# A diffusion and expert kernel on one core: inverse roots by Newton's steps, the first pair of tiles projected ahead of the edges, two PSUM banks for the first layer

## The chip, the cores and the metric

The kernel runs on one core of a Trainium2 chip. The metric is the device time of one execution in microseconds (us), less being better. A core has five engines with a queue each: TensorE (PE in the profile, with PEld for its weight loads), VectorE (DVE), ScalarE (ACT), GpSimd (POOL) and SyncE (SP), which issues transfers. An engine works through its own queue in order and waits for the others by semaphores.

## What is computed

x has 3125 rows of 256 numbers, and a graph of 103,125 edges joins the rows. The first half normalises each row, sends it through a linear layer, a silu, six steps of averaging over the graph and a second linear layer; the second half is a mixture of eight experts with two chosen for each row.

```python
x = x + gnn(layernorm(x), src, dst)      # first half
#   h = silu(layernorm(x) @ W_in.T + b_in)
#   term = h; out = h
#   for i in 1..6:  term = inv_deg * segment_sum(term[src], dst) / i;  out += term
#   gnn = out @ W_out.T + b_out
x = x + moe(layernorm(x))                # second half: top 2 of 8 experts
```

The averaging is linear, so the kernel applies W_out ahead of it: it diffuses rows of 256 already projected numbers, t0.

## The kernel before

The rows lie in 25 tiles of 128 (`NT`, the last one with 53 rows). The work has these stages.

*Prologue, to 96 us.* It has two strands that share all engines. The edges' strand takes source and destination of every edge (`si`, `di`, loaded on ACT's queue), turns them into three small numbers (`part`, L417 to L427), transposes them on PE (L433), copies them out of PSUM (`pairs`, L436 and L437) and writes them to DRAM (`edges`, two writes from ACT's queue, L439 and L441). POOL gathers, by indirect transfers, a row of destinations for each group of rows (`row_i`, L455) and then the edges of the group (`rec`, L471). From these, DVE and ACT work out where each row's edges begin (L474 to L506), the inverse degrees (L510 to L515, the last of it five multiplications on POOL), and the two arrays `place` and `lane` (L527 to L536) from which the adjacency blocks are made. The rows' strand normalises x and projects it. x comes by SP's queue in five pieces (L322), tiles 0 to 1, 2 to 5, 6 to 11, 12 to 17 and 18 to 23. Mean and variance are taken on DVE (L556, L557); the inverse root is ACT's Sqrt (L558) and DVE's reciprocal (L559), in three batches: tiles 0 to 1, 2 to 5, 6 to 24. Sqrt and silu need different tables in ACT, and a table load stands in ACT's queue where the function changes. Then come 13 pairs of tiles: `xn` on ACT (L567), four transposes on PE into `pt` (L572), `xt` copied out by ACT (L579), `ph` = the first layer in two halves on PE (L586), each followed by a silu on ACT into `ht` (L588), `pm` = the output layer on PE (L593), and `t0` in two parts on DVE, the high part rounded to the fp32r type (L595) and what is left of it (L596). `ph` and `pm` have one buffer each, `pt` two. The xn of the next pair is written ahead of the present pair's layers.

*Step 1.* For each of the 25 destination tiles a dense block of the adjacency matrix is built: DVE makes one-hot arrays `left` (L638) and `right` (L647), PE multiplies them into `pa` (L658, 40 matmuls a block), ACT copies `pa` into `blk` (L662), SP writes the block to DRAM. 25 matmuls of the block with t0 then give the tile's sum `pd` (L703). The first blocks' one-hot matmuls are interleaved with the projection; the first L703 needs the whole t0.

*Steps 2 to 6, the router and the experts* load the blocks again (L1014) and do the second half (L954, L963). They begin after step 1.

The source's order sets each engine's queue, except that the scheduler which builds the program moves instructions between strands within each engine by its own estimate of when their inputs are ready; `tc.issue_after(x)`, which the changed kernel uses, holds what is written under it behind instruction x in that order. The projection's loop, which the change rewrites, is in the function printed below.

Of the kernel before, what the change touches and what calls it, by code (L numbers as in the profile page):

```python
# [10 lines left out]
F32 = mybir.dt.float32  # L11
F16 = mybir.dt.float16
F32R = mybir.dt.float32r
BF16 = mybir.dt.bfloat16
I32 = mybir.dt.int32
U32 = mybir.dt.uint32
AF = mybir.ActivationFunctionType
ALU = mybir.AluOpType
AX = mybir.AxisListType

P = 128
N = 3125
D = 256
NT = 25
# [3 lines left out]
NCH = (NE + P - 1) // P  # L28
# [4 lines left out]
STEPS = 6  # L33
# [3 lines left out]
EPS = 1e-5  # L37
# [3 lines left out]
NG = NT * P // W // 2  # L41
# [225 lines left out]
def tile_gnn_then_moe(  # L267
# [20 lines left out]
    nc = tc.nc  # L288

    const = ctx.enter_context(tc.tile_pool(name="const", bufs=1))  # L290
    work = ctx.enter_context(tc.tile_pool(name="work", bufs=2))
# [9 lines left out]
    prep = before.enter_context(tc.tile_pool(name="prep", bufs=1))  # L301
# [2 lines left out]

    acc = const.tile([P, NT, D], F32, name="acc")
    nc.vector.memset(acc[:, NT - 1, :], 0.0)
    first_i = prep.tile([NG, NCH], I32, name="first_i")
    di = prep.tile([P, NCP], I32, name="di")
    nc.scalar.dma_start(di, dst_pm)
    w_in_sb = const.tile([P, 2, D], F32, name="w_in_sb")  # L310
    nc.scalar.dma_start(w_in_sb, w_in.rearrange("(k p) o -> p k o", p=P))
    si = prep.tile([P, NCP], I32, name="si")
    nc.scalar.dma_start(si, src_pm)
    b_in_pm = const.tile([P, 2], F32, name="b_in_pm")
    for c in range(2):
        nc.scalar.dma_start(b_in_pm[:, c:c + 1], b_in[c * P:(c + 1) * P].rearrange("(p a) -> p a", a=1))
    w_out_sb = const.tile([P, 2, D], F32, name="w_out_sb")
# [3 lines left out]
    for a, b in ((0, 2), (2, 6), (6, 12), (12, 18), (18, 24)):  # L321
        nc.sync.dma_start(acc[:, a:b, :], x[a * P:b * P, :].rearrange("(t p) d -> p t d", p=P))  # L322
        if a == 0:
            nc.sync.dma_start(first_i, bass.AP(tensor=dst_pm.tensor, offset=dst_pm.offset,
                                               ap=[[0, NG], [1, NCH]]))
    for p in (0, HP):
        nc.sync.dma_start(acc[p:p + LAST, NT - 1, :], x[(NT - 1) * P:N, :])

    ident = const.tile([P, P], F32, name="ident")
    make_identity(nc, ident)  # L330
    eps_sb = const.tile([P, 1], F32, name="eps_sb")
    nc.vector.memset(eps_sb, EPS)
    inv_deg = const.tile([P, STEPS, NT], F32, name="inv_deg")
    big = const.tile([1, 1], I32, name="big")


# [6 lines left out]
    t0 = evens.enter_context(tc.tile_pool(name="even", bufs=1, side="right")).tile(  # L343
        [P, NT, 2 * D], F32R, name="t0")
# [33 lines left out]
    low = keys.tile([NG, 2], F32, name="low")  # L378
# [33 lines left out]
    nc.vector.tensor_copy(ident_h, ident)  # L412


    cb = (NCP + P - 1) // P
    part = prep.tile([P, 3, NCP], F16, name="part")
    nc.vector.tensor_scalar(part[:, 2, :], di, -MID, None, op0=ALU.add)  # L417
# [10 lines left out]
    pairs = prep.tile([P, cb, P, 3], F16, name="pairs")  # L428
    for v in range(3):
        pq = ps.tile([P, 1024], F16, name="pk")[:, :cb * P].rearrange("p (c e) -> p c e", e=P)  # L430
        for c in range(cb):
            n = min(P, NCP - c * P)
            nc.tensor.transpose(pq[:n, c, :], part[:, v, c * P:c * P + n], ident_h)  # L433
        n = NCP - (cb - 1) * P
        put = nc.vector.tensor_copy if v == 1 else nc.scalar.copy
        put(pairs[:, :cb - 1, :, v], pq[:, :cb - 1, :])  # L436
        put(pairs[:n, cb - 1, :, v], pq[:n, cb - 1, :])  # L437
    by_chunk = edges.rearrange("(c p) v -> c p v", p=P)
    nc.scalar.dma_start(by_chunk[:(cb - 1) * P].rearrange("(b c) p v -> c b p v", c=P),  # L439
                        pairs[:, :cb - 1])  # L440
    nc.scalar.dma_start(by_chunk[(cb - 1) * P:], pairs[:NCP - (cb - 1) * P, cb - 1])  # L441


    junk = prep.tile([P, NCH], BF16, name="junk")
    below = prep.tile([NG, 2], F32, name="below")
    for g in range(2):
        nc.vector.tensor_scalar(junk[:NG, :], first_i, low[:, g:g + 1], None, op0=ALU.is_lt,
                                op1=ALU.add, accum_out=below[:, g:g + 1])
    chunk = prep.tile([NG, 2], F32, name="chunk")
    nc.vector.tensor_scalar(chunk, below, -1.0, 0.0, op0=ALU.add, op1=ALU.max)  # L450
    chunk_i = prep.tile([NG, 2], U32, name="chunk_i")
    nc.vector.tensor_copy(chunk_i, chunk)
    row_i = prep.tile([NG, 2, P], I32, name="row_i")
    for g in range(2):
        nc.gpsimd.indirect_dma_start(  # L455
            row_i[:, g, :], None, dst_cm,
            bass.IndirectOffsetOnAxis(ap=chunk_i[:, g:g + 1], axis=0))
    within = prep.tile([NG, 2], F32, name="within")
    for g in range(2):
        nc.vector.tensor_scalar(junk[:NG, :P], row_i[:, g, :], low[:, g:g + 1], None,  # L460
                                op0=ALU.is_lt, op1=ALU.add, accum_out=within[:, g:g + 1])
    start_i = prep.tile([NG, 2], U32, name="start_i")
    nc.vector.scalar_tensor_tensor(start_i, chunk, float(P), within, op0=ALU.mult, op1=ALU.add)

# [5 lines left out]
    for g in range(2):  # L470
# [4 lines left out]
                                op0=ALU.subtract, op1=ALU.min)  # L475
        nc.vector.scalar_tensor_tensor(pl_f[:, g, :], in_w[:, g, :], float(NT), rec[:, g, :, 1],
                                       op0=ALU.mult, op1=ALU.add)
# [5 lines left out]
    for g in range(2):  # L483
        for a in range(2):
# [3 lines left out]
                            op0=ALU.min)  # L488
# [4 lines left out]
    for g in range(2):  # L493
        nc.scalar.activation(seen[:NG, :], in_w[:, g, :CAP], AF.Sign, bias=w_half, scale=-1.0,
                             accum_out=inside[:, g:g + 1])
    nc.vector.tensor_scalar(begin[:, :, W], inside, 0.5, CAP / 2.0, op0=ALU.mult, op1=ALU.add)
    for d in (1, 2, 4, 8, 16):
        least = keys.tile([NG, 2, W + 1], F32, name=f"least{d}")
        n = W + 1 - d
# [9 lines left out]
    for g in range(2):  # L509
        nc.tensor.matmul(pg, deg_at[:, g].rearrange("p a i -> p (a i)"), in_tile[:, g, :],  # L510
                         start=(g == 0), stop=(g == 1))
# [29 lines left out]
    ps_a = build.enter_context(tc.tile_pool(name="ps_a", bufs=2, space=bass.MemoryType.PSUM,  # L541
                                            reuse_waits="tile"))

    intro = ExitStack()
    proj = intro.enter_context(tc.tile_pool(name="proj", bufs=1, side="right"))
    ps_o = intro.enter_context(tc.tile_pool(name="ps_o", bufs=1, space=bass.MemoryType.PSUM, side="right"))
    ps_t = intro.enter_context(tc.tile_pool(name="ps_t", bufs=2, space=bass.MemoryType.PSUM, side="right"))
    mv = const.tile([P, NT, 2], F32, name="mv")  # L550
    rstd = const.tile([P, NT], F32, name="rstd")
    shift = const.tile([P, NT], F32, name="shift")
    for a, b in ((0, 2), (2, 6), (6, NT)):
        for t in range(a, b):
            st = work.tile([P, 6], F32, name="st")
            nc.vector.bn_stats(st, acc[:, t, :])  # L556
            nc.vector.bn_aggr(mv[:, t, :], st)  # L557
        nc.scalar.activation(rstd[:, a:b], mv[:, a:b, 1], AF.Sqrt, bias=eps_sb, scale=1.0)  # L558
        nc.vector.reciprocal(rstd[:, a:b], rstd[:, a:b])  # L559
        nc.vector.scalar_tensor_tensor(shift[:, a:b], mv[:, a:b, 0], -1.0, rstd[:, a:b],  # L560
                                       op0=ALU.mult, op1=ALU.mult)

    def normed(t):
        n = min(2, NT - t)
        xn = proj.tile([P, 2, D], F32, name="xn")
        for q in range(n):
            nc.scalar.activation(xn[:, q, :], acc[:, t + q, :], AF.Identity,  # L567
                                 bias=shift[:, t + q:t + q + 1], scale=rstd[:, t + q:t + q + 1])
        pt = ps_t.tile([P, 2, 2 * P], F32, name="pt")
        for k in range(2):  # L570
            for q in range(n):
                nc.tensor.transpose(pt[:, k, q * P:(q + 1) * P], xn[:, q, k * P:(k + 1) * P], ident)  # L572
        return pt

    pt = normed(0)
    for t in range(0, NT, 2):
        n = min(2, NT - t)
        xt = proj.tile([P, 2, 2 * P], F32, name="xt")
        nc.scalar.copy(xt[:, :, :n * P], pt[:, :, :n * P])  # L579
        if t + 2 < NT:  # L580
            pt = normed(t + 2)
        ph = ps_o.tile([P, 2, 2 * P], F32, name="ph")
        ht = proj.tile([P, 2, 2 * P], F32, name="ht")
        for c in range(2):
            for k in range(2):
                nc.tensor.matmul(ph[:, c, :n * P], w_in_sb[:, k, c * P:(c + 1) * P], xt[:, k, :n * P],  # L586
                                 start=(k == 0), stop=(k == 1))
            nc.scalar.activation(ht[:, c, :n * P], ph[:, c, :n * P], AF.Silu,  # L588
                                 bias=b_in_pm[:, c:c + 1], scale=1.0)
        pm = ps_o.tile([P, 2, D], F32, name="pm")  # L590
        for q in range(n):
            for c in range(2):
                nc.tensor.matmul(pm[:, q, :], ht[:, c, q * P:(q + 1) * P], w_out_sb[:, c, :],  # L593
                                 start=(c == 0), stop=(c == 1))
        nc.vector.tensor_copy(t0[:, t:t + n, :D], pm[:, :n, :])  # L595
        nc.vector.tensor_sub(t0[:, t:t + n, D:], pm[:, :n, :], t0[:, t:t + n, :D].bitcast(F32))  # L596
    intro.close()
    ps_1 = build.enter_context(tc.tile_pool(name="ps_1", bufs=2, space=bass.MemoryType.PSUM,
                                            reuse_waits="tile"))
# [99 lines left out]
    for j in range(NT):  # L699
        ahead = build_tile(j + 1) if j + 1 < NT else None  # L700
        pd = ps_1.tile([P, 2 * D], F32, name="pd")
        for i in range(NT):
            nc.tensor.matmul(pd, blk[:, i * P:(i + 1) * P], t0[:, i, :],  # L703
                             start=(i == 0), stop=(i == NT - 1))
# [295 lines left out]
    for step in range(2, STEPS + 1):  # L1000
# [5 lines left out]
        for j in range(NT):  # L1006
# [5 lines left out]
            for i in [*range(NT - 2), NT - 1, NT - 2]:  # L1012
                n = D if i == NT - 1 else 2 * D
                nc.tensor.matmul(pd[:, :n], blk[:, i * P:(i + 1) * P], old[:, i, :n],  # L1014
                                 start=(i == 0), stop=(i == NT - 2), skip_group_check=True)
# [24 lines left out]
    with tc.tile_pool(name="sum", bufs=NT // S) as sums:  # L1040
        both = []
        for t in range(0, NT, S):
            for k in range(2):
                got = sums.tile([P, S, D], F32, name=f"got{k}")
                n = S if t + S < NT else S - 1
# [3 lines left out]
                if n < S:  # L1049
                    a = k * YK + (NT - 1) * P  # L1050
# [52 lines left out]
```

## Time and profile before

| | |
|---|---|
| median of 9 runs | 1343.13 us |
| lowest and highest | 1341.26 and 1359.73 us |
| the profiled execution's own time | 1343.57 us |
| its span | 1341.7 us |
| mean granted TensorE clock | 0.967 |
| PE busy | 1231.1 us, 92% of the span |
| start of the first pair's first layer (L586) | 20.73 us |
| start of the last pair's first layer | 89.15 us |
| start of the first aggregation (L703) | 96.27 us |

A row of the timeline has the start, the busy time, the engine, the line, the operation, what it writes and reads with the shapes, a count where neighbours of one kind are put together, and in brackets how long the engine stood idle before it and whose signal ended that. In the table of stretches each row gives the busy time and the number of instructions of each engine, then the granted clock of PE, the share of the transfer engines and the rate. Times in the span start at 0; 1.87 us of the execution lie outside it.

### The profile page before, as it was taken

The numbers are of one execution on the slowest core, as the hardware profiler recorded it, in microseconds if no ns is written. First come the engines' busy times: TensorE is split into PE (matmuls) and PEld (weight loads), VectorE is DVE, ScalarE is ACT, GpSimd is POOL, SyncE is SP. The second block draws the span as 40 slices with busy tenths as digits, with TensorE's granted clock in tenths as the row PEclk, the third lists the DMA queues.
The fourth block names the chain that finished last, engine by engine and source line by source line (L and its number), as shares of the span: only waits on it lengthen the run. The fifth ranks groups of instructions, "written<-read, shape, count | busy, mean of one in ns | idle before, by whom it ended". The sixth has DMA issues, their size and how long they took to land. (4 is left out here: it accounts for less than half of the span.)

```text
span 1341.7 us, 16667 instructions
## 1 busy us (share of the span) xinstructions
PE 1231.1 (92%) x6181; PEld 1016.0 (76%) x6181; DVE 583.9 (44%) x1436; ACT 347.2 (26%) x534; POOL 209.1 (16%) x264
## 2 busy tenths in 40 slices
PE   4999999999999999999999999999999559999940
PEld 3778888887888888888888888887777348888830
DVE  6769999994432222222222222245555412121206
ACT  5656667673000000000000000012222112222210
POOL 2000000007952200000000000001332222222210
PEclk9899999999999999999999999999999879999975
DMA  6014343436988888888888888887888277777737
GB/s 196 1 73 173 148 196 148 197 148 261 350 293 296 294 294 295 296 295 293 295 295 296 293 295 295 295 293 260 284 283 273 77 205 233 223 237 235 229 96 257
DMA packets 86245, 318.47 MB, mean 237 GB/s; under 512 B 12253, under 2 KB 56236, under 8 KB 66952
## 3 DMA queue, kind: packets, MB, share of 16 engines
q1 hardware_dynamic: 74550, 297.14, 63.0%
q0 software_dynamic: 5280, 14.54, 3.2%
q10 hardware_dynamic: 6322, 5.60, 1.3%
q8 instruction: 52, 0.85, 0.2%
q14 instruction: 41, 0.34, 0.1%
HBM read 256.44 MB, written 60.81 MB: 236 GB/s over the span
## 5 line engine op out<-in xcount | busy, mean ns | idle before, releaser
L1014 PE MATMUL pd<-t,blk 128*128 128x512 f32 (+1 forms) x3125 | 713.2, 388 | 2.5 <-DMA blk<-adj 2.5
L1014 PEld LDWEIGHTS pd<-t,blk 128*128 128x128 f32 x3125 | 575.5, 188 | 119.8 <-issue 2.9
L677 DVE SCALAR_TENSOR_TENSOR term<-pd,inv_deg,low 128x256 f32<-128x256 f32 x150 | 72.4, 483 | 451.0 <-ACT low L675 450.8
L675 ACT ACTIVATE low<-pd,inv_deg 128x256 f32<-128x256 f32 x150 | 71.1, 474 | 648.6 <-PE pd L1014 576.7
L703 PE MATMUL pd<-t,blk 128*128 128x512 f32 x625 | 151.1, 398 | 0.0
L662 ACT CAST blk<-pa 128x800 fp32r<-128x800 f32 x98 | 146.8, 1652 | 12.2 <-PE pa L658 12.2
L703 PEld LDWEIGHTS pd<-t,blk 128*128 128x128 f32 x625 | 116.0, 189 | 25.2
L647 DVE TENSOR_TENSOR right<-steps,place 128x800 bf16<-128x800 f16 (+3 forms) x245 | 128.2, 582 | 3.3 <-PE pa L658 3.3
L954 PE MATMUL ph<-xt,w_sb 128*128 128x256 f32 x432 | 99.6, 384 | 2.4 <-DMA w_sb<-in_w_dram 1.3
L658 PE MATMUL pa<-right,left 128*128 128x200 bf16 (+3 forms) x980 | 98.9, 254 | 0.9 <-ACT blk L662 0.9
L963 PE MATMUL py<-w_sb,ht 128*128 128x256 f32 x432 | 97.7, 380 | 0.0
L658 PEld LDWEIGHTS <-left 128*128 128x128 bf16 x980 | 83.4, 97 | 16.4 <-DVE right L647 5.7
L954 PEld LDWEIGHTS ph<-xt,w_sb 128*128 128x128 f32 x432 | 83.1, 193 | 14.3 <-DVE xt L946 3.0
L956 ACT ACTIVATE ht<-ph,b_sb 128x256 f32<-128x256 f32 x108 | 51.0, 473 | 143.8 <-PE ph L954 143.8
L963 PEld LDWEIGHTS py<-w_sb,ht 128*128 128x128 f32 x432 | 80.3, 190 | 9.7
L693 POOL TENSOR_TENSOR early<-t 128x256 f32<-128x256 f32 x50 | 37.6, 762 | 266.6 <-DVE right L647 264.8
L967 POOL DMA_INDIRECT ys<-y,xr x54 | 51.8, 959 | 162.2 <-DVE y L966 161.1
L638 DVE TENSOR_TENSOR left<-steps,lane 128x2560 bf16<-128x2560 f16 x49 | 72.8, 1487 | 1.1 <-PE pa L658 1.1
L946 DVE COPY xt<-px 128x512 f32<-128x512 f32 x27 | 18.7, 692 | 110.1 <-PE px L943 109.8
L848 POOL DMA_INDIRECT xs<-xg,to x50 | 48.8, 977 | 104.4 <-DVE m L787 37.0
L746 POOL IOTA lane_f<- 128x1 f32 x1 | 0.1, 137 | 415.3 <-PE pd L1014 415.3
L687 DVE TENSOR_TENSOR acc<-acc,term 128x256 f32<-128x256 f32 x125 | 55.8, 446 | 0.9
(198 smaller groups left out, 637.5 us busy)
## 6 DMA issues: line engine op xcount, KB each, us to landing
blk<-adj SPq DMA_DIRECT2D x125, 1600.0 KB, 6.8
adj<-blk SPq DMA_DIRECT2D x25, 1536.0 KB, 5.2
w_sb<-in_w_dram SPq DMA_DIRECT2D x54, 512.0 KB, 5.5
xr<-xs SPq DMA_DIRECT2D x27, 257.0 KB, 3.0
got<-ys SPq DMA_DIRECT2D x8, 640.0 KB, 7.1
b_sb<-in_b_dram SPq DMA_DIRECT2D x27, 128.0 KB, 5.1
out_dram<-acc ACTq DMA_DIRECT2D x24, 128.0 KB, 5.0
xs<-pad SPq DMA_DIRECT2D x9, 257.0 KB, 6.2
```

Source lines behind the costliest of these rows:

```text
L638: nc.vector.tensor_tensor(left.rearrange("p k a l u -> p (k a) l u"), steps[:, None, :P, :].to_broadcast([P, nl, P, 2]), lane[:, h, :, :]. ...
L647: nc.vector.tensor_tensor(r, steps[:, None, :m, :].to_broadcast([P, HALF // 2, m, 2]), place[:, h, k, :].rearrange("p (a u) -> p a u", u=2 ...
L658: nc.tensor.matmul(pa[:, u, lo * NT:hi * NT], left[:, k, a, :, u], right[k][:, a, :, u], start=(k == 0), stop=(k == CK - 1), skip_group_ch ...
L662: nc.scalar.copy(by_dst[:, q:q + 2 * W, :].rearrange("p (u q) i -> p u q i", u=2), pa[:, :, :W * NT].rearrange("p u (q i) -> p u q i", i=NT))
L675: nc.scalar.activation(low, pd[:, D:], AF.Copy, scale=inv)
L677: nc.vector.scalar_tensor_tensor(term, pd[:, :D], inv, low, op0=ALU.mult, op1=ALU.add)
L687: nc.vector.tensor_add(acc[:, j, :], acc[:, j, :], term)
L703: nc.tensor.matmul(pd, blk[:, i * P:(i + 1) * P], t0[:, i, :], start=(i == 0), stop=(i == NT - 1))
L954: nc.tensor.matmul(ph, got[1][:, k, q * P:(q + 1) * P], xt[:, k, :], start=(k == 0), stop=(k == 1))
L963: nc.tensor.matmul(py, ht[:, q, h * P:(h + 1) * P], got[2][:, q, :], start=(q == 0), stop=(q == HT - 1))
L967: nc.gpsimd.indirect_dma_start(ys_at[2 * i + h], bass.IndirectOffsetOnAxis(ap=got[0][:, h, D:].bitcast(U32), axis=0), y, None)
L1014: nc.tensor.matmul(pd[:, :n], blk[:, i * P:(i + 1) * P], old[:, i, :n], start=(i == 0), stop=(i == NT - 2), skip_group_check=True)
```

## The change

It has three parts, all in the prologue, and each moves some other work.

1. The inverse root is computed without ACT: from the bits of variance plus epsilon a first guess (shift right by one, subtract from 0x5f3759df), then three of Newton's steps, r = r (1.5 - 0.5 v r r). The tiles 0 to 1 and 2 to 5 are done on DVE, the batches 6 to 11, 12 to 17 and 18 to 24 on POOL, except the shift, the subtraction and the final product with the mean, which stay on DVE. Sqrt is gone from ACT, and one silu on a constant at the very start loads ACT's table ahead of the loads on ACT's queue.
2. The projection becomes a function, `project(t)`. `project(0)` stands ahead of the edges' `part` work, behind the two counts of `below`; the edges' first operations are held behind its last first-layer matmul and silu, and the copies into `pairs` behind the second batch's norms. The counts and the gather of `row_i` are written ahead of it.
3. `ph` takes two PSUM banks, one for each half, and the transposes' `pt` has one buffer in place of two. The high part of t0 is copied on ACT (new L499) in place of DVE; DVE keeps the subtraction (new L500).

In the built program ACT's queue of a steady pair runs: silu of half 1, xt of the next pair, t0 copy of this pair, two xn, silu of the next pair's half 0, perhaps a block's copy.

```diff
+    table = nc.scalar.activation(inv_deg[:, 0, :1], eps_sb, AF.Silu)
+    loads = ExitStack()
+    loads.enter_context(tc.issue_after(table.ins))
     first_i = prep.tile([NG, NCH], I32, name="first_i")
     di = prep.tile([P, NCP], I32, name="di")
-    nc.scalar.dma_start(di, dst_pm)
     w_in_sb = const.tile([P, 2, D], F32, name="w_in_sb")
     nc.scalar.dma_start(w_in_sb, w_in.rearrange("(k p) o -> p k o", p=P))
+    nc.scalar.dma_start(di, dst_pm)
...
+    ps_t = intro.enter_context(tc.tile_pool(name="ps_t", bufs=1, space=bass.MemoryType.PSUM, side="right"))
...
+    def norms(a, b):
+        on = nc.vector if a < 6 else nc.gpsimd
+        for t in range(a, b):
+            st = work.tile([P, 6], F32, name="st")
+            nc.vector.bn_stats(st, acc[:, t, :])
+            nc.vector.bn_aggr(mv[:, t, :], st)
+        v = proj.tile([P, b - a], F32, name=f"v{a}")
+        on.tensor_scalar(v, mv[:, a:b, 1], EPS, None, op0=ALU.add)
+        half = proj.tile([P, b - a], I32, name=f"half{a}")
+        nc.vector.tensor_scalar(half, v.bitcast(I32), 1, None, op0=ALU.arith_shift_right)
+        r = rstd[:, a:b]
+        nc.vector.tensor_scalar(r.bitcast(I32), half, -1.0, float(0x5f3759df), op0=ALU.mult, op1=ALU.add)
+        q = proj.tile([P, b - a], F32, name=f"q{a}")
+        for _ in range(3):
+            on.tensor_tensor(q, r, r, op=ALU.mult)
+            if on is nc.vector:
+                on.scalar_tensor_tensor(q, q, -0.5, v, op0=ALU.mult, op1=ALU.mult)
+                on.scalar_tensor_tensor(r, q, 1.5, r, op0=ALU.add, op1=ALU.mult)
+            else:
+                on.tensor_tensor(q, q, v, op=ALU.mult)
+                on.tensor_scalar(q, q, -0.5, 1.5, op0=ALU.mult, op1=ALU.add)
+                on.tensor_tensor(r, r, q, op=ALU.mult)
+        return nc.vector.scalar_tensor_tensor(shift[:, a:b], mv[:, a:b, 0], -1.0, r,
+                                              op0=ALU.mult, op1=ALU.mult)
...
+    batches = {2: 6, 6: 12, 12: 18, 18: NT}
+    last, seconds = [norms(0, 2)], []
+    turned = [normed(0)]
+    def project(t):
+        n = min(2, NT - t)
+        pt = turned.pop()
+        xt = proj.tile([P, 2, 2 * P], F32, name="xt")
+        nc.scalar.copy(xt[:, :, :n * P], pt[:, :, :n * P])
+        if t + 2 in batches:
+            with tc.issue_after(seconds[-1].ins) if seconds else ExitStack():
+                seconds.append(norms(t + 2, batches[t + 2]))
+        if t + 2 < NT:
+            turned.append(normed(t + 2))
+        ph = ps_o.tile([P, 2, 512], F32, name="ph")
...
+        nc.scalar.copy(t0[:, t:t + n, :D], pm[:, :n, :])
+        nc.vector.tensor_sub(t0[:, t:t + n, D:], pm[:, :n, :], t0[:, t:t + n, :D].bitcast(F32))
...
+    with tc.issue_after(last[0].ins):
+        project(0)
+    behind = ExitStack()
+    for one in last[:3]:
+        behind.enter_context(tc.issue_after(one.ins))
     cb = (NCP + P - 1) // P
     part = prep.tile([P, 3, NCP], F16, name="part")
...
-        put(pairs[:, :cb - 1, :, v], pq[:, :cb - 1, :])
-        put(pairs[:n, cb - 1, :, v], pq[:n, cb - 1, :])
+        with tc.issue_after(seconds[0].ins):
+            put(pairs[:, :cb - 1, :, v], pq[:, :cb - 1, :])
+            put(pairs[:n, cb - 1, :, v], pq[:n, cb - 1, :])
...
-    ps_t = intro.enter_context(tc.tile_pool(name="ps_t", bufs=2, space=bass.MemoryType.PSUM, side="right"))
...
-    for a, b in ((0, 2), (2, 6), (6, NT)):
...
-        nc.scalar.activation(rstd[:, a:b], mv[:, a:b, 1], AF.Sqrt, bias=eps_sb, scale=1.0)
-        nc.vector.reciprocal(rstd[:, a:b], rstd[:, a:b])
...
-        ph = ps_o.tile([P, 2, 2 * P], F32, name="ph")
...
-        nc.vector.tensor_copy(t0[:, t:t + n, :D], pm[:, :n, :])
...
+    for t in range(2, NT, 2):
+        project(t)
```

## The prediction, made before the changed kernel had run

> **What bounds the kernel now.** I read the page first, then busy times by stretch, then the timeline of the prologue, then the waits inside one steady pair of tiles. "New L…" is a line of the changed kernel, plain "L…" one of the kernel before. The page, span and slices:
>
> ```profile
> span 1341.7 us, 16667 instructions
> ...
> PE 1231.1 (92%) x6181; PEld 1016.0 (76%) x6181; DVE 583.9 (44%) x1436; ACT 347.2 (26%) x534; POOL 209.1 (16%) x264
> ...
> PE   4999999999999999999999999999999559999940
> ...
> PEclk9899999999999999999999999999999879999975
> ```
>
> The reader is to see that PE is busy in every slice but the first (a 4) and the router and the tail. The same by stretch; the columns are the stretch, its length, busy time and instruction count of PE, PEld, DVE, ACT and POOL, then the granted clock, the DMA share and GB/s:
>
> ```profile
> 0.00:20.00 20.00, 4.29 (x25) 2.78 (x25) 11.58 (x67) 7.72 (x11) 5.73 (x14) 1.00 0.82 254
> 20.00:45.00 25.00, 19.47 (x83) 14.76 (x84) 19.31 (x77) 16.96 (x33) 4.11 (x7) 0.86 0.20 61
> ...
> 57.00:89.00 32.00, 31.38 (x155) 24.10 (x154) 15.08 (x24) 17.12 (x32) 0.00 (x0) 1.00 0.00 1
> ...
> 97.00:340.00 243.00, 240.54 (x1561) 199.39 (x1561) 207.87 (x350) 148.01 (x117) 29.60 (x41) 0.99 0.47 186
> ```
>
> From 57 us on PE has work beside its waits (the blocks' one-hot matmuls L658 fill them), and from 97 us it is simply full. The change touches nothing behind the first aggregation (L703), so its whole effect is the shift of that one start. It begins at 96.27 us and then repeats every 9.62 us; the POOL row below it prices small POOL operations:
>
> ```profile
> 43.67 1.97 POOL L515 TENSOR_SCALAR inv_deg<-inv_deg 128x25 f32<-128x25 f32 x5 [15.42 <-DVE inv_deg L513]
> ...
> 96.27 6.06 PE L703 MATMUL pd<-t,blk 128*128 128x512 f32 x25
> ...
> 105.90 6.05 PE L703 MATMUL pd<-t,blk 128*128 128x512 f32 x25
> ```
>
> Now the head of the prologue. Times are start and busy time; the bracket is idle time before and who ended it:
>
> ```profile
> 8.03 1.28 ACT L558 ACT_TABLE_LOAD   x1 [8.03 <-DMA first_i<-in_dst_pm_dram]
> ...
> 20.73 2.08 PE L586 MATMUL ph<-xt,w_in_sb 128*128 128x256 f32 x4 [2.50 <-ACT xt L579]
> ...
> 21.69 1.28 ACT L588 ACT_TABLE_LOAD   x1
> ...
> 26.59 1.28 ACT L558 ACT_TABLE_LOAD   x1
> ...
> 30.60 1.28 ACT L588 ACT_TABLE_LOAD   x1
> ...
> 32.42 1.13 PE L586 MATMUL ph<-xt,w_in_sb 128*128 128x256 f32 x4 [3.19 <-ACT ht L588]
> ```
>
> Four table loads, and the first pair's projection starts only at 20.73. The pairs start at 20.73, 28.21, 38.59, 45.42, and from 55.93 every 4.745 us, the last at 89.15. One steady pair:
>
> ```profile
> 61.80 0.47 ACT L588 ACTIVATE ht<-ph,b_in_pm 128x256 f32<-128x256 f32 x1 [2.10 <-PE ph L586]
> ...
> 62.33 0.73 PEld L586 LDWEIGHTS ph<-xt,w_in_sb 128*128 128x128 f32 x4 [0.36 <-ACT ht L588]
> ...
> 63.50 0.47 ACT L588 ACTIVATE ht<-ph,b_in_pm 128x256 f32<-128x256 f32 x1 [0.23 <-PE ph L586]
> ...
> 64.02 1.16 PEld L593 LDWEIGHTS pm<-w_out_sb,ht 128*128 128x128 f32 x6 [0.41 <-ACT ht L588]
> ...
> 66.55 0.47 ACT L588 ACTIVATE ht<-ph,b_in_pm 128x256 f32<-128x256 f32 x1 [2.10 <-PE ph L586]
> ```
>
> A pair is a ring: silu of half 0, half 1's matmuls (62.33, held 0.36 by that silu), silu of half 1, output matmuls (64.02), next pair's half 0 (65.42), silu (66.55). ACT's other work, xn (1.09 at 62.18) and xt (0.58 at 63.87), lies beside PE; the t0 cast and subtraction (0.69 each) are on DVE.
>
> **The change by parts,** as four terms on the start of the first L703. I laid out each engine's queue of both built programs with the rows' durations; for the kernel before this gives pair starts within 0.65 us of the trace and the first L703 at 97.37 for 96.27.
>
> Term 1, pair 0's start. Newton on DVE is 13 dependent small operations at about 0.20 (small L617 to L620 starts 0.18 apart, L512 to L513 0.22; bounds 0.14 to 0.27): 2.6 us, from the mean and variance at 7.1 to 9.7, where now the reciprocal and shift end at 13.2. The one table load left moves ahead of ACT's DMA issues, delaying each by about 1.3 and hidden by transfers that pair 0 doesn't need before 13. But ACT now issues b_in's second half and b_out behind waits for x's first two pieces (landings 6.40 and 11.04) before it may do xn, so xn starts at 10.5 to 11.1, not 9.7. Then xn 1.09, transposes 1.1, xt 0.58: pair 0 at 13.4 to 14.0, taken 13.7. Term: 13.7 - 20.73 = **-7.0**.
>
> Term 2, pair 0 to pair 1. PE is still cold (2.08 for the 4 half-0 passes; 1.03 from 28.21 on): 2.08 + 0.47 + 2.08 + 0.47 + 2.7 (six cold passes) + hand-overs 0.2 = 8.0. Then ACT in order: t0 copy 0.58, the pairs copies 1.45 + 0.40 that stood ahead of pair 0 before, xt 0.58, hand-overs: 3.1. Sum 11.1 against 28.21 - 20.73 = 7.48: **+3.6**. The edges' DMA writes move from 18.91 and 19.41 to about 26.4 and 26.9 on ACT's queue; row_i's gather is issued earlier (13.8 for 18.57), rec's later on POOL (about 31.6 for 25.93) behind the edges and behind a batch's Newton steps in POOL's order. SP's x loads keep their order.
>
> Term 3, pairs 1 to 12. The t0 cast moves from DVE to ACT (new L499) and waits there for the whole output matmul; behind it in ACT's queue stand the next-but-one xn's and then the next pair's half-0 silu. So what was beside PE is now in the ring: half-1 silu 0.52, last three output matmuls 1.57 + 0.04, t0 copy 0.49, xn 0.98, silu 0.51, half-1 matmuls 1.14 + 0.04 = 5.29; with a block cast between the silus 5.55. The copy is priced by xt's row (0.58, also 512 elements from PSUM; 0.49 as back-to-back rows overlap by 0.09). It writes the fp32r type, and the only ACT row that does, L662, takes 1652 ns for 800, or 1.06 for 512; on DVE the same cast costs what a plain copy does (668 and 692 ns), so I stay with 0.58 and keep 0.47 to 1.06. Eleven periods: 5 x 5.29 + 6 x 5.55 = 59.8. Besides, in the early pairs: Newton of tiles 6 to 11 on POOL, whose result an xn ahead of pair 1's half-1 silu needs: 12 x 0.33 = 4.0 (L515's five start 0.33 apart on average; near end 0.19, L480's copy; far end 0.63, its slowest). The casts and counts of the edges on ACT (L479 0.72, L494 0.92) twice: 3.3. Pairs 4 and 5 behind the later rec: 2. Sum 69.1 against 89.15 - 28.21 = 60.94: **+8.2**. The other POOL batches are hidden: their xn's come over 3 us later in the laid-out order.
>
> Term 4, pair 12 to the first L703. PE has 17 one-hot matmuls left there, not 42, as its longer waits swallow them earlier: 25 x 0.098 (40 take 3.9) and the 0.71 wait at 95.36 go: **-3.1**.
>
> The third part, two banks for the halves, I cost at 0: in the built program half 1's first matmul still waits for half 0's silu of the same pair, as in the kernel before. The single transpose buffer that pays for it costs nothing either: xt empties it about 2 us before the next transposes.
>
> Rule against row: each steady pair shows PE held 0.36 there. The Trainium skill, "PSUM — Partial Sum Buffer", section "PSUM bank collisions raise a hardware error", says that accesses of two engines to different banks run clean, so half 1 need not wait; by it alone the sum would be 0.53 x 11 = 5.8 less, but the wait is in the program.
>
> Sum: -7.0 + 3.6 + 8.2 - 3.1 = +1.7. The profiled run took 1343.57 (span 1341.7 and 1.87 around it), which is 0.44 above the median: 1343.13 + 1.7 = **1344.8**.
>
> **Rivals.**
>
> *Faster: the lead survives.* Ring and waits stay short, so that much of the 7 us of term 1 reaches L703. If the ring is 4.745 as before, term 3 shrinks by 59.8 - 52.2 = 7.6: 1344.8 - 7.6 = 1337.2. For it: the ACT queue is only 17.12 of 32 busy at 57 to 89. Against it: ACT's order, in which silu cannot pass the copy.
>
> *Slower: POOL.* The mechanism is Newton on POOL for tiles 6 to 24, 36 dependent operations. At 0.46 a step the laid-out order gives 4.8 us more than at 0.33, at 0.56 8.5 more: 1349.6 to 1353.3. Each 0.01 costs 0.37, so from 0.42 on it carries the time out of the forecast's own range. For it: dependent steps may show more than L515's independent ones, and the 629 ns row at 45.005 beside L647 (two SBUF inputs, 44.93). Against: the other four are 275 to 313.
>
> If every step of the first batch took the 0.63, 12 x 0.30 = 3.6 would be added. The Trainium skill, "SBUF — State Buffer", section "Who interferes with whom", speaks against Newton on POOL here: a DVE instruction with two SBUF inputs shuts out a GpSimd instruction that reads SBUF, and the 629 ns row agrees. By that rule the first batch, the one on the path, meets no such DVE instruction, so it would add 0.
>
> *Slower: the fp32r copy* at 1.06: 0.48 x 12 = 5.8 more, 1350.6.
>
> *The change doesn't do what it says:* true of the two banks, and in the sum already.
>
> **How the numbers follow.** Forecast, 1342 to 1348: 0.47. Lead survives, 1337 to 1342: 0.25. POOL, 1348 to 1354: 0.17. Copy: 0.06. Anything else: 0.05. The range 1338.0 to 1352.5 leaves out the far ends of both sides. About 1% (13.4 us) is what a measurement of this kernel can tell from no change; no case reaches it alone, so faster 0.02, slower 0.04, same 0.94.
>
> **What would show it.** Pair 0's first layer (new L487) near 13.7, pair 1's near 25, a steady period of 5.3 to 5.6 with the t0 copy between two silus on ACT, PE still waiting about 0.36 for half 0's silu, POOL steps near 0.33, the last pair near 94 to 95, first aggregation at 96 to 100. A period near 4.75, POOL steps over 0.45 or a copy over 0.8 would make it wrong, each by its rival.

## The result, and the profile after

| | kernel before | changed kernel |
|---|---|---|
| median | 1343.37 us (78 runs) | 1344.39 us (25 runs) |
| ratio, 95% interval | | 1.0016, 0.9996 to 1.0036 |
| profiled run, its span | 1343.57, 1341.7 | 1344.23, 1342.4 |
| first layer of pair 0, 1, 12 | 20.73, 28.21, 89.15 | 13.81, 25.06, 91.51 |
| first, third aggregation | 96.27, 115.52 | 95.30, 114.51 |
| first matmul of step 2 | 330.16 | 329.68 |

No difference that can be measured, as forecast; 1344.8 was predicted. The seven microseconds by which the first pair starts earlier are nearly all given back before the first aggregation: 0.97 of them is left there and 0.48 at step 2. Behind that point the two profiled runs scatter by more than this (the changed one takes 1.2 longer over steps that the change does not touch), so the sign of the total stays open.

The busy times of the changed kernel by stretch (columns as in the prediction):

```profile
0.00:20.00 20.00, 6.93 (x18) 4.59 (x19) 12.89 (x81) 5.84 (x10) 6.92 (x15) 1.00 0.83 256
20.00:45.00 25.00, 17.58 (x82) 12.42 (x81) 15.62 (x52) 15.98 (x31) 7.93 (x27) 0.93 0.20 59
...
57.00:89.00 32.00, 30.38 (x176) 24.09 (x175) 20.21 (x36) 24.17 (x45) 0.15 (x1) 1.00 0.13 52
...
97.00:340.00 243.00, 240.16 (x1560) 198.89 (x1558) 206.73 (x347) 147.76 (x117) 30.14 (x41) 0.99 0.47 188
```

PE gained 2.6 us of work in the first 20 us (6.93 for 4.29) and lost 1.9 in the next 25 (17.58 for 19.47) and 1.0 from 57 to 89. The idle time was not removed but moved. The head of the prologue in the timeline of the changed kernel:

```profile
0.73 1.28 ACT L311 ACT_TABLE_LOAD   x1 [0.73 <-PEq L1139]
...
11.09 1.09 ACT L461 ACTIVATE xn<-acc,shift,rstd 128x256 f32<-128x256 f32 x2 [8.86 <-DMA b_in_pm<-in_b_in_dram]
...
13.81 2.07 PE L487 MATMUL ph<-xt,w_in_sb 128*128 128x256 f32 x4 [0.68 <-ACT xt L477]
...
25.06 1.13 PE L487 MATMUL ph<-xt,w_in_sb 128*128 128x256 f32 x4
...
31.63 0.17 DVE L454 SCALAR_TENSOR_TENSOR shift<-mv,rstd 128x6 f32<-128x6 f32 x1 [3.40 <-POOL rstd L453]
...
31.97 1.09 ACT L461 ACTIVATE xn<-acc,shift,rstd 128x256 f32<-128x256 f32 x2 [3.11 <-DVE shift L454]
```

The one table load stands at 0.73, beside the first transfers; xn of pair 0 stands behind ACT's DMA issues until 11.09, although its shift is ready at 7.36 (Newton on DVE ran from 4.82); ACT then loses 3.11 in pair 1 behind POOL's Newton. One steady pair of the changed kernel:

```profile
76.03 0.60 PE L466 MATMUL pt<-ident,xn 128*128 128x128 f32 x4
...
76.22 0.59 ACT L499 CAST t<-pm 128x512 fp32r<-128x512 f32 x1 [1.18 <-PE pm L497]
...
76.46 1.03 PE L487 MATMUL ph<-xt,w_in_sb 128*128 128x256 f32 x4
76.72 1.09 ACT L461 ACTIVATE xn<-acc,shift,rstd 128x256 f32<-128x256 f32 x2
...
77.72 0.46 ACT L489 ACTIVATE ht<-ph,b_in_pm 128x256 f32<-128x256 f32 x1
78.08 1.55 ACT L710 CAST blk<-pa 128x800 fp32r<-128x800 f32 x1
...
78.23 0.73 PEld L487 LDWEIGHTS ph<-xt,w_in_sb 128*128 128x128 f32 x4 [0.25 <-ACT ht L489]
...
81.78 1.03 PE L487 MATMUL ph<-xt,w_in_sb 128*128 128x256 f32 x4
```

The order forecast for ACT is there: copy, two xn, silu, and PE held for half 0's silu before half 1 (the 0.25). The period, from half 0 of one pair to half 0 of the next, is 5.30 (71.16, 76.46, 81.78), against 4.745 before. Which of these rows makes it longer is told behind the experiments.

### The profile page after: what moved, and what is told of

It is laid out like the page before. It is cut to its first block, busy times and chain, and to the rows that moved or that the text cites. A ratio compares the mean times of both kernels' runs of the same rounds, so it can differ in the third digit from the quotient of the medians.

```text
span 1342.4 us, 16738 instructions
## 1 busy us (share of the span) xinstructions
PE 1230.6 (92%) x6181; PEld 1014.0 (76%) x6181; DVE 580.6 (43%) x1452; ACT 348.2 (26%) x542; POOL 219.3 (16%) x303
```

## The experiments

The chips differ by more than one per cent, so each kernel is compared by its ratio to the kernel before, run beside it on the same chip, and by starts read from its trace, which agreed to 0.4 between the changed kernel's two traces. The experiments ran in three groups of four; the medians of the kernel before were 1363.47 beside the group without part 3, with t0's copy on DVE, with the halves apart and with Newton on DVE; 1358.43 beside the changed kernel again, without part 1 and the two versions with Newton on DVE and tiles apart; 1360.71 beside the other four. In the table, "pair 12" is the start of the last pair's first layer, "third" that of the third aggregation and "step 2" that of its first matmul.

| kernel | pair 12 | first aggregation | third | step 2 | ratio, 95% interval |
|---|---|---|---|---|---|
| before | 89.15 | 96.27 | 115.52 | 330.16 | 1 |
| changed, again | 91.19 | 94.98 | 114.18 | 329.85 | 0.9989, 0.9974 to 1.0004 |
| part 1 alone, on before | 89.41 | 95.09 | 117.09 | 331.91 | 1.0019, 0.9993 to 1.0046 |
| part 2 alone (t0 copy on ACT) | 93.50 | 97.88 | 117.08 | 331.83 | 1.0027, 0.9997 to 1.0057 |
| part 3 alone, on before | 94.36 | 98.85 | 117.70 | 332.45 | 1.0016, 0.9995 to 1.0038 |
| without part 1 (Sqrt) | 95.07 | 98.77 | 117.59 | 332.28 | 1.0031, 1.0001 to 1.0061 |
| without part 3 (one bank) | 89.33 | 95.82 | 118.33 | 333.45 | 1.0038, 1.0003 to 1.0073 |
| t0 copy back on DVE | 95.78 | 101.34 | 120.56 | 335.81 | 1.0006, 0.9979 to 1.0032 |
| halves in tiles apart | 81.35 | 90.34 | 113.96 | 328.28 | 0.9974, 0.9948 to 1.0001 |
| Newton all on DVE | 86.70 | 90.93 | 110.11 | 324.88 | 0.9967, 0.9932 to 1.0003 |
| Newton on DVE, without part 3 | 83.23 | 89.70 | 112.26 | 327.00 | 0.9985, 0.9957 to 1.0014 |
| Newton on DVE, tiles apart | 75.75 | 82.83 | 107.59 | 321.96 | 0.9941, 0.9921 to 0.9960 |
| the same and t0 on DVE | 81.04 | 87.30 | 106.50 | 321.33 | 0.9940, 0.9919 to 0.9962 |

The starts of the first aggregation mislead where one-hot matmuls of the second block are left over: 80 one-hot matmuls come before it in the kernel before, in the changed one and in three others (82 with t0's copy back on DVE), but only 48 or 60 in five, and 99 or 100 without part 1 and with part 3 alone. The third aggregation, by which the same blocks have been built, orders the kernels as step 2 does. Alone, each part comes to step 2 some 1.7 to 2.3 later than the kernel before; together they come 0.5 earlier. Parts 1 and 3 without part 2 were not run.

The time does not follow these starts closely. From step 2 on the kernels' instructions are the same, yet the profiled executions on the other chips took 1023.1 to 1032.3 for them (1041.4 in the changed kernel run again, where PE stands 12.34 once in step 2). So the starts tell what the prologue does, and only the ratios tell the time: t0's copy back on DVE starts step 2 5.6 later than the kernel before, and its ratio is 1.0006.

**The changed kernel again.**

> The changed kernel itself, run again beside the next three. Theory 'equal': its first aggregation starts within 0.5 of 95.30 us and the clock is halved once, for some 3.4 us behind PE's idle time at 26 to 28.5; the ratio to the kernel before lies in 0.999 to 1.003. Rival 'chip': on a chip whose kernel before is slower, further halvings of the clock come inside the prologue, and the first aggregation moves by 3 or more.

Equal: first aggregation at 94.98, one stretch with a halved clock (mean 0.57 at 28 to 32). The interval holds 1.

**The halves in two tiles.** The wait that the change left in is taken away:

```diff
-        ph = ps_o.tile([P, 2, 512], F32, name="ph")
+        ph = [ps_o.tile([P, 512], F32, name=f"ph{c}") for c in range(2)]
...
-                p = nc.tensor.matmul(ph[:, c, :n * P], w_in_sb[:, k, c * P:(c + 1) * P], xt[:, k, :n * P],
+                p = nc.tensor.matmul(ph[c][:, :n * P], w_in_sb[:, k, c * P:(c + 1) * P], xt[:, k, :n * P],
...
-            h = nc.scalar.activation(ht[:, c, :n * P], ph[:, c, :n * P], AF.Silu,
+            h = nc.scalar.activation(ht[:, c, :n * P], ph[c][:, :n * P], AF.Silu,
```

> The changed kernel with the first layer's halves in two tiles of one bank each in place of one tile of two banks; in its built program half 1's matmuls no longer wait for half 0's silu. Theory 'ring' (the projection's ring of PE and ACT sets the first aggregation, and its start sets the end): the ring loses 0.53 in eleven periods, the steady period falls from 5.30 to 4.3 to 4.8, the first aggregation starts at 89.5 to 91 (changed kernel: 95.30), and the time is 4.5 to 6 less than the changed kernel's. Rival 'blocks': the first aggregation is as early, but DVE has not got the next blocks' one-hot arrays ready, the second to fifth aggregations come later than 9.62 apart, and only 1 to 2.5 us are left of it. Rival 'no wait there': the wait of 0.36 was covered by other work and nothing moves by more than 0.5.

The period fell to 4.29, and the eight passes of both halves run in one go; the first aggregation starts at 90.34, 5.0 earlier, as the ring theory had it. Yet only 0.6 of that is left at the third aggregation and 1.4 at step 2. That is as the rival "blocks" had it: 60 one-hot matmuls, not 80, come before the first aggregation, and the next two aggregations start 12.0 and 11.6 later, not 9.6. Besides, the pairs lose time on the way, which rows of the timeline and the clock in stretches of 4 us show:

```profile
56.25 1.89 PE L487 MATMUL ph<-xt,w_in_sb 128*128 128x256 f32 x8
...
58.20 0.17 DVE L454 SCALAR_TENSOR_TENSOR shift<-mv,rstd 128x7 f32<-128x7 f32 x1 [2.68 <-POOL rstd L453]
...
58.45 1.09 ACT L461 ACTIVATE xn<-acc,shift,rstd 128x256 f32<-128x256 f32 x2 [1.85 <-DVE shift L454]
...
60.79 0.98 PE L497 MATMUL pm<-w_out_sb,ht 128*128 128x256 f32 x2 [2.54 <-ACT ht L489]
```

```profile
56.00:60.00 4.00, 2.25 (x13) 1.68 (x11) 1.80 (x4) 2.14 (x5) 1.59 (x8) 1.00 0.00 0
60.00:64.00 4.00, 3.21 (x9) 2.41 (x10) 3.35 (x9) 1.18 (x4) 0.00 (x0) 0.63 0.01 4
64.00:68.00 4.00, 4.00 (x21) 3.12 (x20) 0.91 (x3) 2.90 (x6) 0.00 (x0) 0.95 0.00 0
```

The faster pairs catch up with POOL's last Newton batch, for which no xn waited in the changed kernel. ACT waits for its shift, PE stands 2.54 us, and for some 3.4 us behind that its clock is halved (means of 0.63 and 0.95): that one pair takes 8.58, not 4.29.

**One bank again, two transpose buffers.**

```diff
-    ps_t = intro.enter_context(tc.tile_pool(name="ps_t", bufs=1, space=bass.MemoryType.PSUM, side="right"))
+    ps_t = intro.enter_context(tc.tile_pool(name="ps_t", bufs=2, space=bass.MemoryType.PSUM, side="right"))
...
-        ph = ps_o.tile([P, 2, 512], F32, name="ph")
+        ph = ps_o.tile([P, 2, 2 * P], F32, name="ph")
```

> The changed kernel with its third part undone: both halves of the first layer in one bank, two buffers for the transposes. Theory 'ring': half 1 waits for half 0's silu in both programs, so the period stays at 5.3, the first aggregation within 0.7 of 95.30 and the time within 1 of the changed kernel's. Rival 'transposes': with two buffers the next pair's transposes no longer stand behind the copy of the last, the period falls to about 4.75 and the first aggregation to 94 to 94.6, time about 1 less.

The ring went as the rival said: 4.75, with the t0 copy still on ACT. So the third part had lengthened it. The time did not follow: here too the pairs meet POOL's last batch (shift at 59.38 after 2.68 of waiting on DVE, PE idle 2.09 at 59.8, pair 6 to 7 takes 7.74, with a clock of 0.88 and 0.69 in the stretches 60 to 64 and 64 to 68), and 20 of the one-hot matmuls fall behind the first aggregation.

**Newton on DVE alone.**

```diff
-        on = nc.vector if a < 6 else nc.gpsimd
+        on = nc.vector
```

> The changed kernel with all of Newton's steps on DVE (POOL does none). Theory 'ring': ACT's idle time of 3.11 behind the shift in pair 1 shrinks, since 11 dependent steps on DVE at 0.20 take 2.2 where POOL with its hand-overs took 4.1; the first aggregation starts 1.5 to 2 earlier, at 93.3 to 93.8, and the time falls by as much. Rival 'DVE full': DVE's steps delay the edges' work and the one-hot arrays by 3 x 2.2, the gain is lost in pairs 4 to 6, first aggregation 95 to 97.

It gained more than expected, 4.4 at the first aggregation and 4.8 at step 2. ACT's queue at the same place:

```profile
27.40 0.45 ACT L489 ACTIVATE ht<-ph,b_in_pm 128x256 f32<-128x256 f32 x1
29.21 1.09 ACT L461 ACTIVATE xn<-acc,shift,rstd 128x256 f32<-128x256 f32 x2 [1.36 <-DVE shift L454]
30.21 0.46 ACT L489 ACTIVATE ht<-ph,b_in_pm 128x256 f32<-128x256 f32 x1
```

1.36 of waiting in place of 3.11 makes 1.75. Another 1.0 is there already at pair 1 (24.06 for 25.06), ahead of every Newton step of POOL: the last six output passes of pair 0 took 2.01, not 2.87. The theory has no term for that, and the changed kernel's second trace is 0.3 apart from its first at the same place. The rest comes later: pair 2 to 3 takes 5.30, not 5.86, pair 5 to 6 5.60, not 6.78, and the first one-hot matmul starts at 51.13, not 54.57. In pair 5 to 6 the changed kernel's DVE stands 2.41 behind POOL's last batch:

```profile
57.18 0.17 DVE L454 SCALAR_TENSOR_TENSOR shift<-mv,rstd 128x7 f32<-128x7 f32 x1 [2.41 <-POOL rstd L453]
```

No xn waits for this shift, but the one-hot arrays stand behind it in DVE's queue, and PE waits for them (0.97 and 0.37).

**t0's copy back on DVE.**

```diff
-        nc.scalar.copy(t0[:, t:t + n, :D], pm[:, :n, :])
+        nc.vector.tensor_copy(t0[:, t:t + n, :D], pm[:, :n, :])
```

> The changed kernel with the copy of t0's high part back on DVE. Theory 'ring': the copy of 0.49 leaves the ring, so the steady period falls from 5.30 to about 4.8, the first aggregation starts at 91 to 93, time 2 to 4.5 less. Rival 'DVE full': DVE gets 12 x 0.69 = 8.3 more work in the stretch in which it also makes the first blocks' one-hot arrays; its queue holds the arrays back behind the output matmul, the period stays over 5.2 and the first aggregation starts at 96 to 99, time 0.5 to 3 more.

The ring theory fell here. The copy is gone from ACT and the period is still 5.30. Steady rows of this kernel:

```profile
75.02 0.60 PE L466 MATMUL pt<-ident,xn 128*128 128x128 f32 x4
75.22 0.69 DVE L499 CAST t<-pm 128x512 fp32r<-128x512 f32 x1
...
75.72 1.09 ACT L461 ACTIVATE xn<-acc,shift,rstd 128x256 f32<-128x256 f32 x2 [0.21 <-PE pt L466]
...
76.72 0.45 ACT L489 ACTIVATE ht<-ph,b_in_pm 128x256 f32<-128x256 f32 x1
```

xn overwrites the one buffer that the transposes read. They run after the output matmuls, so xn can start only when they end, whether or not a copy stands ahead of it: the copy lay beside the transposes. And DVE, as the rival said, now holds the one-hot arrays back (first one-hot matmul at 58.71) and waits behind POOL again (the clock is 0.66 at 36 to 40, 0.76 at 64 to 68 and 0.82 at 68 to 72); the first aggregation is later even than the rival's 96 to 99.

**Part 3 alone, on the kernel before.**

```diff
-    ps_t = intro.enter_context(tc.tile_pool(name="ps_t", bufs=2, space=bass.MemoryType.PSUM, side="right"))
+    ps_t = intro.enter_context(tc.tile_pool(name="ps_t", bufs=1, space=bass.MemoryType.PSUM, side="right"))
...
-        ph = ps_o.tile([P, 2, 2 * P], F32, name="ph")
+        ph = ps_o.tile([P, 2, 512], F32, name="ph")
```

> The kernel before with the third part alone: two banks for the halves, one buffer for the transposes, t0's copy still on DVE. Theory 'ring': half 1 still waits for half 0's silu, and with one buffer for the transposes the two xn stand ahead of half 0's silu in ACT's queue, so the steady period is 4.75 to 5.3, the first aggregation 0 to 3 later than 96.27, time 0 to 3 more. Rival 'banks': the wait of 0.36 is gone, period below 4.5, time 2 or more less.

Period 5.35 to 5.39 with the copy on DVE. In the table of waits at 57 to 90 of this kernel the second line is new: ACT's xn waits for the transposes. The table of before at the same place has lines like the first and the third, but none like this:

```profile
DVE t L595 <- PE pm L593: 12.7, 6, 3.8
ACT xn L567 <- PE pt L572: 5.3, 4, 1.7
...
PEld ph L586 <- ACT ht L588: 1.6, 6, 0.3
```

The wait of half 1 for half 0's silu (last line) is still there with two banks in one tile.

**Part 1 undone, and part 1 alone.** Undone:

```diff
-    table = nc.scalar.activation(inv_deg[:, 0, :1], eps_sb, AF.Silu)
-    loads = ExitStack()
-    loads.enter_context(tc.issue_after(table.ins))
...
-        v = proj.tile([P, b - a], F32, name=f"v{a}")
...
         r = rstd[:, a:b]
+        nc.scalar.activation(r, mv[:, a:b, 1], AF.Sqrt, bias=eps_sb, scale=1.0)
+        nc.vector.reciprocal(r, r)
```

> The changed kernel with its first part undone: the inverse roots by ACT's Sqrt and DVE's reciprocal in the same five batches, no early table load; ten table loads of 1.28 stand in ACT's queue. Theory 'ring': the pair 0 start moves from 13.8 to about 15.7, three of the later switches lie in the ring at 2.8 each, less 1.5 to 2 for POOL's chain that is gone; the first aggregation starts at 100 to 103 and the time is 4 to 7 more than the changed kernel's. Rival 'covered': the loads lie beside PE's cold matmuls, the first aggregation starts within 1.5 of the changed kernel's.

First aggregation 98.77, 3.5 later than in the changed kernel and less than forecast: pair 0 is even earlier (12.86), as ACT issues b_out at 7.75, not 10.70, and can begin xn at 10.14; pair 2 to 3, in which two table loads stand and PE idles 5.07, and with it a halved clock (0.63 and 0.51 at 36 to 40 and 40 to 44), takes 11.66, not 5.86. The time, 4.5 more than the changed kernel's beside it, is as forecast. Alone, Newton stands in the kernel before as `norms` above, DVE for tiles 0 to 5 and one POOL batch for 6 to 24:

```diff
-        nc.scalar.activation(rstd[:, a:b], mv[:, a:b, 1], AF.Sqrt, bias=eps_sb, scale=1.0)
-        nc.vector.reciprocal(rstd[:, a:b], rstd[:, a:b])
+        on = nc.vector if a < 6 else nc.gpsimd
...
+        for _ in range(3):
+            on.tensor_tensor(q, r, r, op=ALU.mult)
...
```

> The kernel before with the first part of the change alone: Newton's steps (DVE for tiles 0 to 5, POOL for tiles 6 to 24 in one batch) and the early table load; order of the strands, one bank and two transpose buffers as before. Theory 'ring': pair 0 stays at 19.5 to 20.7, since the copies into pairs stand ahead of its xt on ACT; the silu of pair 1 no longer stands behind two table loads and the Sqrt (31.90), pair 2 starts at 35 to 37 in place of 38.59, the period stays at 4.75, first aggregation at 92.5 to 95, time 1.3 to 3.8 less than the kernel before. Rival 'POOL': the one POOL batch of 19 tiles waits for the last x tiles and is the new wait, pair 2 at 38 to 40, time equal within 1.

The rival came: pair 2 starts at 35.30, but pair 3 waits for the POOL batch (ACT idle 2.36 at 38.8 behind the shift at 40.92), pair 2 to 3 takes 10.66, and nothing is won.

**Part 2 alone** (both other parts undone, with the edits above).

> The changed kernel with its first and its third part undone: pair 0 ahead of the edges, t0's copy on ACT, roots by Sqrt in five batches with ten table loads, one bank and two buffers for the transposes. Theory 'ring': the table loads cost what they cost in the kernel with Sqrt (first aggregation 98.76 there), the period is 4.75 as in the one-bank kernel, so the first aggregation starts at 95 to 98 unless the clock is halved again, and the time is 0 to 3 more than before. Rival 'edges': the edges' strand, now later, is the bound; the first one-hot matmuls start after 56 and the time is 4 or more above before.

As the ring theory had it: pair 0 at 12.82, period 4.75, two pairs of 12.12 with table loads, first aggregation at 97.88.

**Combined versions.** The two edits that helped, "tiles apart" and "Newton on DVE":

> Two edits together on the changed kernel: the halves in two tiles of one bank (no wait of half 1 for half 0's silu) and all of Newton's steps on DVE. Alone, the first gave a period of 4.29 but a stall of 2.5 at 58.2 behind POOL's last batch with a halved clock after it, and the second a first aggregation at 90.93. Theory 'ring': the gains add, the stall at 58 is gone, the first aggregation starts at 83 to 87 and the time is 6 to 9 less than the changed kernel's. Rival 'blocks': the first aggregation starts as early but with fewer of the next block's one-hot matmuls done; the second and third aggregations come 11 to 12 apart, not 9.6, and 2 to 4 less is left than with Newton on DVE alone, or nothing.

and with t0's copy on DVE as well:

> The same two edits and the copy of t0's high part back on DVE. Theory 'ring': one more 0.5 leaves the ring of each pair, so the first aggregation starts 1 to 3 earlier than with the two edits and the time falls by 1 to 2 more. Rival 'DVE full': DVE gets 12 x 0.69 more, the one-hot arrays come later, and the time is 1 to 6 more than with the two edits, as the copy back on DVE alone put the first aggregation at 101.34.

and Newton on DVE without part 3:

> The changed kernel with its third part undone and all of Newton's steps on DVE: one bank, two buffers for the transposes. Theory 'ring': period 4.75 and no POOL wait, the first aggregation starts at 86 to 89 (with Newton on DVE alone: 90.93), time 1 to 4 less than that kernel, 5.5 to 8 less than before. Rival 'blocks': fewer one-hot matmuls are done by then, the second aggregation comes 11 to 12 later, and the time is within 1 of the kernel with Newton on DVE alone (4.5 less than before).

The first two are 0.6% faster than the kernel before (1351.96 and 1350.29 against 1358.43 on the same chip), with intervals that leave 1 out, and the changed kernel's interval on that chip lies above theirs. In both the clock is at 1.00 throughout the prologue, and PE stands longer than 1.5 us once in the first (2.10 at 35.5) and not at all in the second, from pair 1 on. From the first 12.5 us that "tiles apart, Newton on DVE" wins at the first aggregation, 6.9 are left at the third and 7.7 at step 2: rival "blocks" is right in what it says of the size (7.7 is 2.9 more than Newton on DVE alone won there), and the time, 6.2 less than the changed kernel's, is in the ring theory's range too. The waits at 75 to 130 of that kernel:

```profile
ACT blk L710 <- PE pa L706: 6.9, 8, 2.0
...
PE pa L706 <- ACT blk L710: 3.5, 6, 0.9
```

PE and ACT now wait for each other over the blocks' one-hot matmuls and their copies, which the slower kernels had done in the gaps of the ring. With t0's copy on DVE the time is the same by another road: the last line is 0.7 there, and the first aggregation is 4.5 later, where the ring theory had it 1 to 3 earlier. Newton on DVE without part 3 won 5.6 at the first aggregation and 2.7 at step 2; its ratio's interval holds 1.

## Why the prediction was right, and where it was not

That 1344.8 lies 0.4 from the measured 1344.39 is luck: +1.7 was forecast for the first aggregation, -0.97 came, and what lies behind it scatters by more than either. That no difference would be seen was right, and for the reason given, a lead at pair 0 that the pairs behind it give back.

*Term 1 (pair 0 earlier by 7.0):* measured 13.81 - 20.73 = -6.9. Right, also in its reason: Newton's end was not the limit, ACT's issues were (11.09). The table load ahead of them was taken to delay each by 1.3; it was 0.5 (si issued at 2.18 for 1.67). And DVE could begin the first statistics at 3.82, not 6.42, for which no run shows the cause; neither was on the path.

*Term 2 (+3.6):* 11.25 against 7.47, +3.8. Right.

*Term 3 (+8.2):* 91.51 - 25.06 = 66.45 against 60.94, **+5.5. This is the step that failed,** by 2.7, and with it the sign at the first aggregation: -6.9 + 3.8 + 5.5 - 3.3 is -0.9 (measured -0.97), not +1.7. Two sizes were off. A block's copy does not lengthen the ring (5.55 was taken for six periods): it starts 0.1 before the silu ends and runs beside half 1's matmuls, so the steady periods are 5.30 (one is 5.37); and the last two periods are 4.97 and 4.76, the one with a single xn in it and the other with none. 2.4 of the 2.7 are these.

The attribution inside the ring failed too; that its sum came out (5.29 for 5.30) is luck. The prediction put the moved t0 copy into the ring at 0.49 and costed the third part at 0, "the single transpose buffer ... costs nothing either", because the buffer is emptied well before the next transposes. The runs show the reverse: with the copy on DVE the period stays at 5.30, with two transpose buffers it is 4.75 whatever engine copies, and part 3 alone takes the kernel before from 4.75 to 5.37. What the prediction passed over is the order on PE. A steady pair of the kernel before:

```profile
65.42 1.03 PE L586 MATMUL ph<-xt,w_in_sb 128*128 128x256 f32 x4
...
66.28 0.60 PE L572 MATMUL pt<-ident,xn 128*128 128x128 f32 x4
...
66.92 1.09 ACT L567 ACTIVATE xn<-acc,shift,rstd 128x256 f32<-128x256 f32 x2
...
67.07 1.13 PE L586 MATMUL ph<-xt,w_in_sb 128*128 128x256 f32 x4
...
70.17 1.03 PE L586 MATMUL ph<-xt,w_in_sb 128*128 128x256 f32 x4
```

Here the transposes (66.28) run behind half 0, while its silu (66.55) runs, and xn comes behind that silu. In the changed kernel they stand ahead of half 0 (76.03 and 76.46), and xn (76.72) ahead of the silu. From half 1 to the next half 0 it takes 3.55 (78.23 to 81.78) for 3.10 (67.07 to 70.17), and 0.43 of this difference is the time from the first transpose to half 0. From half 0 to its silu it takes 1.26 for 1.13, as xn now stands between. Together these are the 0.57 by which this period (5.32) is longer than that (4.75). The steady pairs of t0's copy back on DVE, part 3 alone and the halves apart, with one buffer each, have the changed kernel's order; those of one bank and part 2 alone, with two, have that of before. No run changed the number of buffers by itself.

*Term 4 (-3.1):* 3.79 for 7.13, -3.3. Right: 17 one-hot matmuls are left there, not 42, and the wait of 0.71 is gone.

*The copy's price* (0.58 taken, 1.06 feared) was 0.59, as for xt in f32: the fp32r type cost ACT nothing here; L662's 1.65 for 800 elements has a cause that was not tried.

*POOL's steps* (0.33 taken): 0.28 apart in the first batch, 0.35 in the second, 0.39 in the third. That rival is the one that the experiments made true: in both kernels whose ring was shortened with Newton still on POOL (the halves apart, one bank), POOL's last batch became the wait. And "hidden" was too strong already in the changed kernel: no xn waited for the later batches, as laid out, but DVE's queue did (the 2.41 at 57.18), and with Newton on DVE the pairs behind the first batch were faster too.

*Faster rival, the wait that two banks should have taken:* priced at 0.53 a pair; a tile for each half took 1.0 off the period (5.30 to 4.29). The Trainium skill's rule ("PSUM — Partial Sum Buffer", "PSUM bank collisions raise a hardware error"), that accesses to different banks run clean, agrees with the run: both halves' eight passes ran in 1.89 with half 0's silu beside them (passes 69.12 to 71.01, silu from 70.39 to 70.84). Two banks in one tile kept the wait (0.25), two tiles of one bank each did not: it was the tile, not the bank, by which the program waited.

What the time behind the first aggregation did stays open: the profiled run lost its lead of 0.48 again after step 2, in stages whose instructions are the same, and on another chip the ratio fell below 1. Both intervals hold 1. The prediction took the shift of the first aggregation for the whole effect; that held in the changed kernel as far as step 2 (-0.97, -1.00 at the third, -0.48), but not in the experiments in which one-hot matmuls were left over.

## What to carry to other kernels

An early start is worth only what the slowest ring behind it keeps: here 6.9 us at the first pair were 0.97 at the first aggregation. Before pricing a moved instruction, see what else the engine behind it waits for; here the copy lay beside the transposes and cost nothing, and one buffer fewer, with the order that came with it, cost 0.55 to 0.6 a pair. When a wait is to be removed by another bank, read in the built program whether it is gone: two tiles did it, two halves of a tile did not.

## What the runs showed of the hardware

PE's clock is halved after some idle stretches in mid-work. In the kernel before PE stands 3.19 us until 32.42 behind the table loads; the clock in the stretches of 4 us from there:

```profile
32.00:36.00 4.00, 2.21 (x7) 1.41 (x8) 4.00 (x11) 4.00 (x10) 0.00 (x0) 0.69 0.00 0
36.00:40.00 4.00, 4.00 (x12) 3.07 (x12) 2.97 (x11) 1.07 (x3) 0.00 (x0) 0.50 0.00 0
```

The mean of 0.50 in the second row is the halved clock itself: some 7 us there, and about 3.4 in the changed kernel after 2.25 of idling at 26.3. So a gap can cost its own length and some of the work behind it. The shortest gap in a prologue with a halved clock after it was 1.95 (t0's copy on DVE, at 64.1). It does not always follow: 2.10 at 35.5 in "tiles apart, Newton on DVE" left the clock at 1.00. What decides it was not tried.

A clock of 1.00 in a row is not always full speed: the changed kernel's row of 0 to 20 shows 1.00, but the four passes of half 0 take 2.07 there (at 13.81) and 1.03 later (at 76.46).

A POOL operation on 7 elements a partition took 1.36 us beside a DVE comparison with two inputs in SBUF, and the eleven that followed 0.20 or 0.21 each. The changed kernel's POOL and DVE rows:

```profile
52.48 1.48 DVE L686 TENSOR_TENSOR left<-steps,lane 128x2560 bf16<-128x2560 f16 x1
```

```profile
52.65 1.36 POOL L446 TENSOR_TENSOR q<-rstd 128x7 f32<-128x7 f32 x1
54.09 0.20 POOL L451 TENSOR_TENSOR q<-q,v 128x7 f32<-128x7 f32 x1
```

That is the exclusion which the Trainium skill states ("SBUF — State Buffer", "Who interferes with whom"): POOL was let go when `left` ended (53.96).
